# A four-layer graph network on one core: first factor, first products and second factor of the last layer are placed anew

## The chip, the cores and the metric

One core of a Trainium2 chip runs one program with five engines that work at once, each through its own list of instructions in order: PE (TensorE, matrix products into PSUM), DVE (VectorE), ACT (ScalarE), POOL (GpSimd) and SP (SyncE, which here only issues loads). PSUM has eight banks of 2 KB per partition; a bank holds 512 numbers of 32 bits for each of 128 partitions. The metric is the device time of the program in microseconds, as the median of several runs.

## The reference, cut to what matters

Four graph layers on 4096 nodes with 64 features and one dense 4096 x 4096 adjacency matrix, each followed by a residual sum and a layer norm: a Chebyshev layer, an attention layer with two gated cells, a decay layer and a hyperbolic layer. The change lies between the last two:

```python
# layer 2: the last 100 neighbours of a row, weighed by halves
rank = jnp.cumsum(mask, axis=1)
k = jnp.minimum(rank[:, -1:], 100.)
pos = rank - (rank[:, -1:] - k)
w = mask * jnp.where(pos > 0, 0.5 ** (k - pos), 0.0)
x = layernorm(x + w @ (x @ weight) + bias)
# layer 3: log map of every node j at every node i, summed over the neighbours
log_ij = logmap(x[:, None, :], x[None, :, :])     # per pair: a norm, an arctanh
agg = jnp.einsum('ij,ijc->ic', adj / deg, log_ij)
x = layernorm(x + expmap(0, agg @ weight + bias))
```

The log map of a pair depends on one number v(i, j), a product of a vector made from x[i] and one made from x[j]; from it follow an arctanh and a square root, made with logarithms and exponentials.

## The kernel before, in words

Rows are taken in eight groups of 512 columns (`GW`), each group being four blocks of 128 nodes. The matrix is transposed on PE in the first layer and kept in device memory (`adj_t`) with a mask (`mask_t`).

**Decay layer** (loop at L1431). It runs in two turns of four groups, groups 4 to 7 first. In each turn PE goes down through 64 half blocks, with four count matmuls per half block (L1450) into the two banks `cnt_ps` of the pool `ps_c2`; ScalarE (L1455), or VectorE for one of two when no other work is queued (`busy`; L1457), turns the counts into bit patterns of powers of two, `wt`; then PE gathers with them into the four banks `acc_ps` (L1410, L1422). Behind the last gather of a turn `copies` (L1476) takes the four sums from PSUM by VectorE (L1479). What ends a group of rows is cut into steps in the list `seam`, one of which is taken per block pair: `ends` (L1343) makes for two groups the product with the weights (L1360, eight matmuls into a `post` bank), the sum and statistics (L1364 to L1372), the root by logarithm (L1375), the norm (L1380 to L1393), then `prepare` (L1271) and `turn_prepared` (L1289), which leave the transposed columns `tr_c`, `tr_o`. The steps of the first turn run beside the second turn; those of the second turn run in the last layer.

**Last layer** (from L1509). The pairs (i, j) of groups with j not before i in the sequence 4, 5, 6, 7, 0, 1, 2, 3 (`seq`) make 36 tiles, each of two halves: 72 half tiles n. For each group i a pair of **right factors** is made once by `right(i)` (L1526): four matmuls of `tr_c` with `to_right` (L1531) and four of `tr_o` with `to_other` go into two `post` banks, and ScalarE copies them to `rv` and `ro` (L1534). A half tile passes through: `product` (L1577, PE, two banks of `v_ps`), `square` (L1586, ACT), `opposite` (L1596, PE, adds into the same banks), `less_one` (L1604, DVE), Ln and Exp (L1801, L1802, ACT), L1826 (DVE, the last reader of `v_ps`), Exp (L1828) and Ln (L1837, ACT), L1811 and L1814 (DVE, the weight times the matrix entry), transposes for the mirrored tile (L1622, L1624), and gathers into `sums_ps` (L1638, L1650).

The order: `in_order` keeps marked instructions of one engine as written; the rest is placed by a scheduler when the program is built. At the start of the last layer the text has `right(4)`, `product(0)`, `square(0)`, `less_one(0)`, `opposite(0)`, `product(1)`, and then the loop. One or two steps of `seam` are taken per round. `right(5)` comes at round 10, six half tiles ahead of its use.

The pools of PSUM lie one behind another. Decay layer: `ps_c2` two banks, `ps_p2` two (`post`), `ps_a2` four (`acc_ps`). Last layer: `ps_v3` two times two banks (`v_ps`), `ps_a3` two, `ps_p3` two. So the first `v_ps` lies on the counts' banks, the second on the old `post` banks, and the new `post` banks on two of the sums. The matrix `tb` collects finished sums; VectorE fills seven parts of it with zeros at the start (L1544), POOL one (L1542).

Of the kernel before, what the change touches and what calls it, by code (L numbers as in the profile page):

```python
# [9 lines left out]
F32 = mybir.dt.float32  # L10
F32R = mybir.dt.float32r
BF16 = mybir.dt.bfloat16
# [3 lines left out]
ALU = mybir.AluOpType  # L16
AX = mybir.AxisListType
PSUM = bass.MemoryType.PSUM
# [10 lines left out]
V_FLOOR = 2.0**-21  # L29
# [11 lines left out]
SCALE = 2.0**-10  # L41
# [21 lines left out]
def gnn4_kernel(  # L63
# [21 lines left out]
    nc = tc.nc  # L85
    P = 128
    N, F = x.shape
    NB = N // P
    GB = 4
    GW = GB * P  # L90
# [10 lines left out]
    def gcols(g):  # L101
        return slice(g * GW, (g + 1) * GW)
# [264 lines left out]
    wq_signed = const.tile([P, 2, H3], F32, name="wq_signed")  # L367
# [157 lines left out]
    with tc.tile_pool(name="acc", bufs=1) as acc_p, tc.tile_pool(  # L525
        name="cols0", bufs=4
    ) as cols_p, tc.tile_pool(name="kept0", bufs=1) as kept_p, tc.tile_pool(name="diag0", bufs=2) as diag_p, tc.tile_pool(
        name="ps_t0", bufs=3, space=PSUM
    ) as ps_t, tc.tile_pool(name="ps_a0", bufs=1, space=PSUM) as ps_a, tc.tile_pool(
        name="ps_p0", bufs=2, space=PSUM  # L530
# [178 lines left out]
        for g in range(NG):  # L709
# [3 lines left out]
            for c in reversed(range(NCH)):  # L713
# [45 lines left out]
                n = g * NCH + c  # L759
# [55 lines left out]
        for g in reversed(range(NG - 1)):  # L815
            ps = ps_a.tile([P, GW], F32, name="pass2", tag=("h_ps", "w_ps")[g % 2])
# [60 lines left out]


    turns_of = [list(range(NG - QG, NG)), list(range(NG - QG))]

    def load2(to, groups, c):

# [456 lines left out]


    decayed = {}

    def ends(two):  # L1343
# [12 lines left out]
        def summed(ps_p):  # L1356
            o = ps_p.tile([P, GB, 2 * F], F32, name="post", tag="post")
            for b in range(GB):
                for q, g in enumerate(two):
                    nc.tensor.matmul(  # L1360
                        o[:, b, q * F : (q + 1) * F], lhsT=decayed[g][:, cols(b)], rhs=wd, start=True, stop=True
                    )
            halves = "p (q b) f -> p q b f"
            nc.vector.tensor_tensor(  # L1364
                x2.rearrange(halves, q=2), o.rearrange("p b (q f) -> p q b f", q=2),
                nat_b[:, bs, :].rearrange(halves, q=2), ALU.add,
            )
            st = sm.tile([P, 2 * GB, 6], F32, name="ln_st")
            for b in range(2 * GB):
                nc.vector.bn_stats(st[:, b, :], x2[:, b, :])  # L1370
                nc.vector.bn_aggr(mv[:, b, :], st[:, b, :])
            nc.vector.tensor_scalar_add(ve, mv[:, :, 1], LN_EPS)  # L1372

        def roots(ps_p):
            nc.scalar.activation(s, ve, AF.Ln)  # L1375
            nc.scalar.activation(s, s, AF.Exp, scale=0.5)

        def rest(ps_p):

# [12 lines left out]
            nc.vector.tensor_scalar_mul(ve, ve, 1.0 / F)  # L1392
            nc.vector.tensor_tensor(x2, x2, over_all(ve), ALU.subtract)  # L1393

        return [summed, roots, rest, lambda ps_p: prepare(two)] + [
            lambda ps_p, g=g: turn_prepared(ps_p, g) for g in two
        ]

    with tc.tile_pool(name="mask2", bufs=3) as mk_p, tc.tile_pool(name="wt2", bufs=3) as wt_p, tc.tile_pool(
# [31 lines left out]
        for turn, groups in enumerate(turns_of):  # L1431
# [9 lines left out]
            for h in reversed(range(2 * NB)):  # L1441
# [31 lines left out]

                gathers += lo + two if jb == 0 else two + lo
                if jb == 0:
                    def copies(ps_p, acc=acc, groups=groups):  # L1476
                        for q, g in enumerate(groups):
                            decayed[g] = three.tile([P, GW], F32, name=f"sums{q}")
                            nc.vector.tensor_copy(decayed[g], acc[q])  # L1479

                    assert turn == 0 or not seam
                    seam += [lambda ps_p: None, copies]
                    for a in range(2):
                        seam += ends((groups[2 * a], groups[2 * a + 1]))
                busy = bool(seam)
                if seam:
                    seam.pop(0)(ps_p)
# [18 lines left out]

    with tc.tile_pool(name="o3", bufs=1) as op, tc.tile_pool(name="cols3", bufs=3) as cols_p, tc.tile_pool(  # L1509
        name="w3", bufs=4  # L1510
    ) as wp3, tc.tile_pool(name="el3", bufs=3) as el, tc.tile_pool(name="f3", bufs=2) as fp, tc.tile_pool(
        name="r3", bufs=2
    ) as rp, tc.tile_pool(name="ps_v3", bufs=2, space=PSUM) as ps_v, tc.tile_pool(
        name="ps_a3", bufs=2, space=PSUM
    ) as ps_a, tc.tile_pool(name="ps_p3", bufs=2, space=PSUM) as ps_p:
        HB = CB // 2

        tb = op.tile([P, N], F32, name="tb")
# [1 line left out]
        spread_w = two_w[:, F : 2 * F]  # L1520
        kappa = op.tile([P, 2, NB], F32, name="kappa")

        rvs = [op.tile([P, GW], F32, name=f"rv{q}") for q in range(2)]
        ros = [op.tile([P, GW], BF16, name=f"ro{q}") for q in range(2)]

        def right(i):  # L1526
            q = seq.index(i) % 2
            for to, w, t in ((rvs[q], to_right, tr_c), (ros[q], to_other, tr_o)):
                ps = ps_p.tile([P, GW], F32, name="post", tag="post")
                for b in range(GB):  # L1530
                    nc.tensor.matmul(  # L1531
                        ps[:, cols(b)], lhsT=w[:, b % 2, :], rhs=t[:, (i * GB + b) // 2, :], start=True, stop=True
                    )
                nc.scalar.copy(to, ps)  # L1534
            return rvs[q], ros[q]


        seq = turns_of[0] + turns_of[1]
        tiles = [(i, j) for n, i in enumerate(seq) for j in seq[n:]]
        NT = len(tiles)  # L1540
        own, mirrored = {}, {}
        nc.gpsimd.memset(tb[F:P, gcols(seq[0])], 0.0)  # L1542
        for g in seq[1:]:
            nc.vector.memset(tb[0:F, gcols(g)], 0.0)  # L1544

        def load_own(t):
            if t < NT and t not in own:
# [12 lines left out]
            i, j = tiles[n // 2]  # L1560
            return slice(2 * P if i == j and n % 2 else 0, GW)

        rights, sums, fs = {}, {}, {}
        vs, ws, rts = {}, {}, {}
        NU = 2 * NT

        def product(n):

            if n >= NU:
                return  # L1570
            i, j = tiles[n // 2]
            vs[n] = ps_v.tile([P, HB, GW], F32, name="v_ps")
            cs = columns(n)
            for k in range(HB):
                jb = j * CB + (n % 2) * HB + k
                half = slice(jb % 2 * F, jb % 2 * F + F)
                in_order(nc.tensor.matmul(  # L1577
                    vs[n][:, k, cs], lhsT=tr_c[half, jb // 2, :], rhs=rights[i][0][half, cs], start=True, stop=True
                ))

        def square(n):
            if n >= NU:
                return
            ws[n] = wp3.tile([P, HB, GW], F32, name="w3")
            cs = columns(n)
            nc.scalar.activation(ws[n][:, :, cs], vs[n][:, :, cs], AF.Square)  # L1586

        def opposite(n):
            if n >= NU:
                return  # L1590
            i, j = tiles[n // 2]
            cs = columns(n)
            for k in range(HB):
                jb = j * CB + (n % 2) * HB + k
                half = slice(jb % 2 * F, jb % 2 * F + F)
                in_order(nc.tensor.matmul(  # L1596
                    vs[n][:, k, cs], lhsT=tr_o[half, jb // 2, :], rhs=rights[i][1][half, cs],
                    start=False, stop=True, skip_group_check=True,
                ))

        def less_one(n):
            if n < NU:
                w = ws[n][:, :, columns(n)]
                nc.vector.tensor_scalar(w, w, -SCALE * SCALE, V_FLOOR * (V_FLOOR + 2.0) * SCALE**2, ALU.add, ALU.max)  # L1604

        def turn(n):

# [171 lines left out]
        for t in range(3):  # L1779
            load_own(t)  # L1780
            load_mirrored(t)
        rights[seq[0]] = right(seq[0])
        product(0)
        square(0)
        less_one(0)
        opposite(0)
        product(1)
        n = 0
        while n < NU + 2 or turns or gathers:
            if n % 2:  # L1790
# [49 lines left out]
            for _ in range(2 if n == 0 else 1):  # L1840
                if seam:
                    seam.pop(0)(ps_p)
            if n + 6 < NU and tiles[(n + 6) // 2][0] not in rights:
                i = tiles[(n + 6) // 2][0]
                rights[i] = right(i)
            n += 1

        before, last = seam[:-6], seam[-5:]
# [49 lines left out]
```

## Time and profile before

| what | us |
|---|---|
| median of three runs | 1402.75 (1402.37 to 1404.16) |
| the profiled execution | 1408.86, its span 1407.1 |
| first weight load of the decay counts (L1450) | 762.5 |
| sums of the second turn copied from | 963.97 |
| last gather of the decay layer ends | 964.15 |
| busy PE, DVE, ACT, POOL over the span | 1310.2, 1052.1, 805.7, 110.5 |

A line of the chain has the start in the span, the length, the engine and the line. A stretch has its bounds and length, each engine's busy time with the number of instructions, the granted clock of PE as a share of the full one, the share of the DMA engines and their rate. fp32 matmuls are recorded in two passes, so four matmuls are eight records. PE's busy time is modelled and does not mean that its array is full.

### The profile page before, as it was taken

The numbers are of one execution on the slowest core, as the hardware profiler recorded it, in microseconds if no ns is written. First come the engines' busy times: TensorE is split into PE (matmuls) and PEld (weight loads), VectorE is DVE, ScalarE is ACT, GpSimd is POOL, SyncE is SP. The second block draws the span as 40 slices with busy tenths as digits, with TensorE's granted clock in tenths as the row PEclk, the third lists the DMA queues.
The fourth block names the chain that finished last, engine by engine and source line by source line (L and its number), as shares of the span: only waits on it lengthen the run. The fifth ranks groups of instructions, "written<-read, shape, count | busy, mean of one in ns | idle before, by whom it ended". The sixth has DMA issues, their size and how long they took to land.

```text
span 1407.1 us, 19039 instructions
## 1 busy us (share of the span) xinstructions
PE 1310.2 (93%) x6790; PEld 611.1 (43%) x6790; DVE 1052.1 (75%) x2015; ACT 805.7 (57%) x1341; POOL 110.5 (8%) x191
## 2 busy tenths in 40 slices
PE   7999999999999999999999999997889898989893
PEld 5655556556544334444444323333333333333341
DVE  7599889999434257788885224356999999999997
ACT  4544434434000115654424675744989999999894
POOL 2111111011123000010111000000000000000000
PEclk9999999999999999999999999997999999999998
DMA  9999999999799999999985755534244354445330
GB/s 317 392 390 412 376 410 400 405 404 384 290 381 372 388 419 373 421 350 340 329 306 179 239 173 165 181 120 180 78 162 187 149 229 158 184 154 198 138 120 12
DMA packets 108191, 382.16 MB, mean 272 GB/s; under 512 B 20276, under 2 KB 20280, under 8 KB 76472
## 3 DMA queue, kind: packets, MB, share of 16 engines
q1 hardware_dynamic: 87096, 296.17, 57.0%
q0 software_dynamic: 12736, 76.29, 13.2%
q10 hardware_dynamic: 8256, 8.39, 1.7%
q8 instruction: 56, 0.92, 0.3%
q14 instruction: 47, 0.39, 0.1%
HBM read 294.05 MB, written 85.20 MB: 270 GB/s over the span
## 4 chain that ended last, share of the span: by engine, by line
PE 59%; ACT 15%; DVE 15%; DMA 6%; issue 3%; SPq 1%; ACTq 0%; POOL 0%; DVEq 0%
PE pass L566 7%; PE tp L723 6%; PE w_ps L566 6%; PE pass L559 4%; PE cnt_ps L1450 4%; PE a_last L1181 4%; PE a_ps L1181 4%; PE acc_ps L1410 3%; DMA raw<-in_adj_dram 3%; PE h_ps L559 3%; ACT w L1801 2%; ACT rt L1802 2%; DVE rt L1826 2%; ACT w L1586 2%; DVE at_m L1624 2%
## 5 line engine op out<-in xcount | busy, mean ns | idle before, releaser
L730 ACT COPY at<-tp 128x512 f32<-128x512 f32 x248 | 128.5, 598 | 124.2 <-issue 88.6
L1455 ACT ACTIVATE wt<-cnt_ps 128x512 uint16<-128x512 f32 x210 | 116.5, 595 | 65.3 <-PE cnt_ps L1450 63.0
L758 DVE TENSOR_REDUCE dpart<-raw 128x4 f32<-128x2048 f32 x64 | 145.4, 2274 | 4.8 <-DMA raw<-in_adj_dram 4.7
L1638 PE MATMUL sums_ps<-at_d,some 128*64 128x512 f32 x288 | 144.3, 621 | 2.7 <-DVE at_d L1617 1.7
L760 DVE TENSOR_REDUCE lows<-raw 128x1 f32<-128x2048 f32 x64 | 145.4, 2272 | 0.0
L723 PE MATMUL tp<-ident,raw 128*128 128x128 f32 x1024 | 134.4, 285 | 9.8 <-DMA raw<-in_adj_dram 8.3
L723 PEld LDWEIGHTS tp<-ident,raw 128*128 128x128 f32 x1024 | 117.8, 146 | 46.8 <-issue 37.3
L1650 PE MATMUL sums_ps<-at_m,some 128*64 128x512 f32 x224 | 110.0, 613 | 0.0
L1577 PE MATMUL v_ps<-rv,tr_a 64*128 64x512 f32 (+1 forms) x288 | 82.6, 652 | 21.1 <-DVE rt L1826 20.8
L566 PE MATMUL pass<-at,cheb_n 128*128 128x512 f32 x224 | 97.5, 593 | 0.5 <-DVE cheb_n L792 0.5
L566 PE MATMUL w_ps<-at,cheb_n 128*128 128x512 f32 x200 | 91.8, 602 | 0.0
L1826 DVE SCALAR_TENSOR_TENSOR rt<-v_ps,rt 128x1024 f32<-128x1024 f32 x72 | 83.2, 1156 | 5.3 <-ACT rt L1802 4.7
L1450 PE MATMUL cnt_ps<-m,follow 128*64 128x512 fp8e4 x480 | 81.7, 391 | 4.6 <-ACT wt L1455 1.5
L1814 DVE TENSOR_TENSOR at_d<-at_d,f 128x1024 f32<-128x1024 f32 x72 | 83.2, 1156 | 0.1
L1811 DVE SCALAR_TENSOR_TENSOR f<-rt,w 128x1024 f32<-128x1024 f32 x72 | 83.1, 1158 | 0.2 <-ACT rt L1837 0.2
L1624 DVE TENSOR_TENSOR at_m<-post,at_m 128x512 f32<-128x512 f32 x112 | 74.9, 680 | 8.6 <-PE post L1622 8.4
L1837 ACT ACTIVATE rt<-rt 128x1024 f32<-128x1024 f32 x72 | 72.1, 1005 | 11.4 <-DVE rt L1826 10.8
L1457 DVE TENSOR_SCALAR wt<-cnt_ps 128x512 uint16<-128x512 f32 x46 | 31.8, 692 | 59.0 <-PE cnt_ps L1450 59.0
L1801 ACT ACTIVATE w<-w 128x1024 f32<-128x1024 f32 x72 | 72.0, 1000 | 6.5 <-DVE w L1604 6.4
L1622 PE MATMUL post<-ident,f 128*128 128x128 f32 x448 | 68.9, 284 | 4.8 <-DVE at_m L1624 4.5
L1828 ACT ACTIVATE w<-w 128x1024 f32<-128x1024 f32 x72 | 72.4, 1006 | 0.6
L1802 ACT ACTIVATE rt<-w 128x1024 f32<-128x1024 f32 x72 | 72.4, 1005 | 0.6
(426 smaller groups left out, 2279.7 us busy)
## 6 DMA issues: line engine op xcount, KB each, us to landing
at<-adj_t SPq DMA_DIRECT2D x119, 1024.0 KB, 8.5
raw<-in_adj_dram SPq DMA_DIRECT2D x64, 1024.0 KB, 13.3
adj_t<-at POOLq DMA_DIRECT2D x62, 1024.0 KB, 8.2
at_d<-adj_t SPq DMA_DIRECT2D x36, 1024.0 KB, 4.6
at_m<-adj_t SPq DMA_DIRECT2D x28, 1024.0 KB, 6.7
m<-mask_t SPq DMA_DIRECT2D x120, 128.0 KB, 2.9
m<-mask_t SPq DMA_DIRECT2D x60, 256.0 KB, 4.2
mask_t<-mask ACTq DMA_DIRECT2D x28, 256.0 KB, 7.5
```

Source lines behind the costliest of these rows:

```text
L566: in_order(nc.tensor.matmul(ps, lhsT=cheb_n[:, jb, k : k + 2, :], rhs=rhs, start=first, stop=last))
L723: in_order(nc.tensor.transpose(tp[:, cols(b)], raw[:, b, cols(k)], ident))
L730: nc.scalar.copy(at[:, k, :], tp)
L758: in_order(nc.vector.tensor_reduce(dpart[:, g, c, :], raw, AX.X, ALU.add))
L760: in_order(nc.vector.tensor_reduce(lows[:, n : n + 1], raw.rearrange("p b j -> p (b j)"), AX.X, ALU.min))
L1181: in_order(nc.tensor.matmul(ps[q * F : (q + 1) * F, :], lhsT=nat_a[:, c * CB + k, 0:F], rhs=of[q if signed else 0][:, k, :], start=(c == 0 ...
L1450: in_order(nc.tensor.matmul(cnt[a][r * HP : (r + 1) * HP, :], lhsT=follow, rhs=chunks[c][odd][2 * a + r][:, k, :], start=(h == 2 * NB - 1) ...
L1455: in_order(nc.scalar.activation(wt[odd][a], cnt[a], AF.Relu, scale=-128.0))
L1624: work.append(lambda to=to, tp=tp: nc.vector.tensor_tensor(to, tp, to, ALU.mult))
L1638: in_order(nc.tensor.matmul(bank[0:F, :], lhsT=nat_c[:, j * CB + k, :], rhs=own[t][:, k, :], start=(i == j and k == 0), stop=(j == seq[-1] ...
L1650: in_order(nc.tensor.matmul(bank[F:P, :], lhsT=nat_c[:, above * GB + k, :], rhs=mirrored[tm][:, k, :], start=(k == 0 and above == seq[0]), ...
L1826: nc.vector.scalar_tensor_tensor(rt, vs[n][:, :, cs], (1.0 + V_FLOOR) * SCALE, rt, ALU.max, ALU.add)
```

## The change

1. `right(seq[0])` is made in the decay layer, as the last step of `seam` in the first turn. Its results lie in places that are there already: `rv` in the unused quarter of the tile `some`, the first `ro` in the weights `wq_signed`. `right` takes the pool as an argument.
2. The pools of the last layer are ordered `ps_v3` (one buffer, two banks: the counts'), `ps_p3` (the old `post` banks), `ps_u3` (one buffer, two banks: sums 0 and 1), `ps_a3` (sums 2 and 3). Even half tiles use `ps_v3`, odd ones `ps_u3`.
3. In the second turn sums 2 and 3 are copied by ScalarE.
4. The order at the start: `product(0)`, `square(0)`, `product(1)`, `less_one(0)`, `opposite(0)`. `behind` makes the first row-end matmuls stand behind the first products and the first `opposite` on PE, and the row-end sum behind `less_one(0)` on DVE, by an edge for the scheduler that is no wait.
5. `right(seq[1])` moves from round 10 to round 0, behind the row-end products.
6. The seven fills of `tb` go to POOL.

```diff
+    rights, begun = {}, {}
+    rvs = [some[:, N // 4 + q * GW : N // 4 + (q + 1) * GW] for q in range(2)]
+    ros = [wq_signed.rearrange("p q h -> p (q h)")[:, 0 : GW // 2].bitcast(BF16)]
+    def right(ps_p, i):
+        q = seq.index(i) % 2
+        for to, w, t in ((rvs[q], to_right, tr_c), (ros[q], to_other, tr_o)):
...
+        rights[i] = rvs[q], ros[q]
+    def behind(engine, ins):
+        if engine in begun:
+            tc.add_manual_dep(
+                ins.ins, begun[engine],
+                mybir.DependencyInfo(mybir.DependencyClass.NoSync, mybir.DependencyReason.DATA),
+                reason="behind",
+            )
+        begun[engine] = ins.ins.name
@@ ends: row-end products and sum @@
+                    if begun:
+                        behind("PE", ins)
...
+            if begun:
+                behind("DVE", ins)
@@ decay layer @@
-                            nc.vector.tensor_copy(decayed[g], acc[q])
+                            copy = nc.scalar.copy if turn and q > 1 else nc.vector.tensor_copy
+                            copy(decayed[g], acc[q])
...
+                    if turn == 0:
+                        seam.append(lambda ps_p: right(ps_p, seq[0]))
@@ last layer @@
-        name="r3", bufs=2
-    ) as rp, tc.tile_pool(name="ps_v3", bufs=2, space=PSUM) as ps_v, tc.tile_pool(
-        name="ps_a3", bufs=2, space=PSUM
-    ) as ps_a, tc.tile_pool(name="ps_p3", bufs=2, space=PSUM) as ps_p:
+    with tc.tile_pool(name="ps_v3", bufs=1, space=PSUM) as ps_v, tc.tile_pool(
+        name="ps_p3", bufs=2, space=PSUM
+    ) as ps_p, tc.tile_pool(name="ps_u3", bufs=1, space=PSUM) as ps_u, tc.tile_pool(name="o3", bufs=1) as op, tc.tile_pool(name="cols3", bufs=3) as cols_p, tc.tile_pool(
...
-            nc.vector.memset(tb[0:F, gcols(g)], 0.0)
+            nc.gpsimd.memset(tb[0:F, gcols(g)], 0.0)
...
-            vs[n] = ps_v.tile([P, HB, GW], F32, name="v_ps")
+            vs[n] = (ps_u if n % 2 else ps_v).tile([P, HB, GW], F32, name="v_ps")
...
+                if n < 2:
+                    behind("PE", ins)
...
+                if n < 1:
+                    behind("PE", ins)
...
+                if n < 1:
+                    behind("DVE", ins)
...
-        rights[seq[0]] = right(seq[0])
         product(0)
         square(0)
+        product(1)
         less_one(0)
         opposite(0)
-        product(1)
...
+            if n == 0:
+                right(ps_p, seq[1])
             if n + 6 < NU and tiles[(n + 6) // 2][0] not in rights:
                 i = tiles[(n + 6) // 2][0]
-                rights[i] = right(i)
+                right(ps_p, i)
```

More of the change, by code (lines that the diff above doesn't have):

```diff
@@ L879, in gnn4_kernel @@
     turns_of = [list(range(NG - QG, NG)), list(range(NG - QG))]
+    seq = turns_of[0] + turns_of[1]
     def load2(to, groups, c):
@@ L1341, in gnn4_kernel @@
     decayed = {}
+    rights, begun = {}, {}
[4 more added lines that the diff above has]
+        for to, w, t in ((rvs[q], to_right, tr_c), (ros[q], to_other, tr_o)):
+            ps = ps_p.tile([P, GW], F32, name="post", tag="post")
+            for b in range(GB):
+                nc.tensor.matmul(
+                    ps[:, cols(b)], lhsT=w[:, b % 2, :], rhs=t[:, (i * GB + b) // 2, :], start=True, stop=True
+                )
+            nc.scalar.copy(to, ps)
+        rights[i] = rvs[q], ros[q]
[5 more added lines that the diff above has]
+                reason="behind",
+            )
+        begun[engine] = ins.ins.name
     def ends(two):
@@ L1359, in summed @@
                 for q, g in enumerate(two):
-                    nc.tensor.matmul(
+                    ins = nc.tensor.matmul(
                         o[:, b, q * F : (q + 1) * F], lhsT=decayed[g][:, cols(b)], rhs=wd, start=True, stop=True
                     )
+                    if begun:
+                        behind("PE", ins)
             halves = "p (q b) f -> p q b f"
-            nc.vector.tensor_tensor(
+            ins = nc.vector.tensor_tensor(
                 x2.rearrange(halves, q=2), o.rearrange("p b (q f) -> p q b f", q=2),
@@ L1475, in gnn4_kernel, with copies @@
                 if jb == 0:
-                    def copies(ps_p, acc=acc, groups=groups):
+                    def copies(ps_p, acc=acc, groups=groups, turn=turn):
                         for q, g in enumerate(groups):
                             decayed[g] = three.tile([P, GW], F32, name=f"sums{q}")
-                            nc.vector.tensor_copy(decayed[g], acc[q])
+                            copy = nc.scalar.copy if turn and q > 1 else nc.vector.tensor_copy
+                            copy(decayed[g], acc[q])
                     assert turn == 0 or not seam
@@ L1493, in gnn4_kernel @@
     staying.close()
-    with tc.tile_pool(name="o3", bufs=1) as op, tc.tile_pool(name="cols3", bufs=3) as cols_p, tc.tile_pool(
+    with tc.tile_pool(name="ps_v3", bufs=1, space=PSUM) as ps_v, tc.tile_pool(
+        name="ps_p3", bufs=2, space=PSUM
+    ) as ps_p, tc.tile_pool(name="ps_u3", bufs=1, space=PSUM) as ps_u, tc.tile_pool(name="o3", bufs=1) as op, tc.tile_pool(name="cols3", bufs=3) as cols_p, tc.tile_pool(
         name="w3", bufs=4
@@ L1512, in gnn4_kernel @@
         name="r3", bufs=2
-    ) as rp, tc.tile_pool(name="ps_v3", bufs=2, space=PSUM) as ps_v, tc.tile_pool(
+    ) as rp, tc.tile_pool(
         name="ps_a3", bufs=2, space=PSUM
-    ) as ps_a, tc.tile_pool(name="ps_p3", bufs=2, space=PSUM) as ps_p:
+    ) as ps_a:
         HB = CB // 2
@@ L1521, in gnn4_kernel @@
         kappa = op.tile([P, 2, NB], F32, name="kappa")
[L1523 to L1538, printed above, removed]
         tiles = [(i, j) for n, i in enumerate(seq) for j in seq[n:]]
@@ L1561, in columns @@
             return slice(2 * P if i == j and n % 2 else 0, GW)
-        rights, sums, fs = {}, {}, {}
+        sums, fs = {}, {}
+        ros.append(op.tile([P, GW], BF16, name="ro1"))
         vs, ws, rts = {}, {}, {}
@@ L1576, in product @@
                 half = slice(jb % 2 * F, jb % 2 * F + F)
-                in_order(nc.tensor.matmul(
+                ins = nc.tensor.matmul(
                     vs[n][:, k, cs], lhsT=tr_c[half, jb // 2, :], rhs=rights[i][0][half, cs], start=True, stop=True
-                ))
+                )
+                in_order(ins)
+                if n < 2:
+                    behind("PE", ins)
         def square(n):
@@ L1595, in opposite @@
                 half = slice(jb % 2 * F, jb % 2 * F + F)
-                in_order(nc.tensor.matmul(
+                ins = nc.tensor.matmul(
                     vs[n][:, k, cs], lhsT=tr_o[half, jb // 2, :], rhs=rights[i][1][half, cs],
                     start=False, stop=True, skip_group_check=True,
-                ))
+                )
+                in_order(ins)
+                if n < 1:
+                    behind("PE", ins)
         def less_one(n):
@@ L1603, in less_one @@
                 w = ws[n][:, :, columns(n)]
-                nc.vector.tensor_scalar(w, w, -SCALE * SCALE, V_FLOOR * (V_FLOOR + 2.0) * SCALE**2, ALU.add, ALU.max)
+                ins = nc.vector.tensor_scalar(
+                    w, w, -SCALE * SCALE, V_FLOOR * (V_FLOOR + 2.0) * SCALE**2, ALU.add, ALU.max
+                )
+                if n < 1:
+                    behind("DVE", ins)
         def turn(n):
```

## The prediction

> **What bounds the kernel now.** I read the order of time first, to find where the decay layer hands over to the last layer, since the change touches only that passage; then the chain of waits there; then the engines' busy time in short stretches on either side.
>
> The chain between 963 and 977 us (start, length, what):
> ```profile
> 963.98 0.28 DVE sums L1479
> ...
> 964.58 1.89 DVE sums L1479 x3
> ...
> 966.51 1.17 PE post L1531 x8
> ...
> 967.75 0.59 ACT rv L1534
> ...
> 968.39 2.08 PE v_ps L1577 x4
> 970.46 3.62 PE post L1360 x16
> 974.10 0.07 DVE nat_a L1364
> ...
> 974.71 0.69 DVE w L1604
> 975.43 1.06 ACT w L1801
> ```
> The reader is to see one work after another: four copies empty the decay sums, then the first right factor is made, copied, used by the first product, then sixteen matmul records of the row ends go ahead, and only then VectorE does the step that lets ScalarE take its first logarithm, at 975.43. The last gather into the sums ended at 964.15 (963.77 + 0.38 in the order of time), so 11.3 us pass.
>
> The stretches (us, then busy PE, weight loads, DVE, ACT, POOL; granted clock; DMA share; GB/s):
> ```profile
> 960.00:964.00 4.00, 4.00 (x40) 1.44 (x37) 1.42 (x4) 1.20 (x2) 0.00 (x0) 1.00 0.00 0
> 964.00:968.00 4.00, 1.64 (x14) 1.27 (x12) 3.84 (x7) 0.25 (x1) 0.52 (x1) 0.95 0.66 248
> 968.00:972.00 4.00, 3.67 (x13) 2.11 (x12) 2.06 (x6) 1.85 (x3) 0.00 (x0) 0.50 1.01 422
> 972.00:976.00 4.00, 3.46 (x16) 2.68 (x16) 1.90 (x9) 0.57 (x1) 0.00 (x0) 0.50 1.02 426
> 976.00:980.00 4.00, 1.10 (x4) 0.60 (x5) 3.59 (x17) 4.00 (x9) 0.00 (x0) 0.50 1.01 418
> 1000.00:1020.00 20.00, 17.15 (x90) 8.06 (x88) 19.97 (x46) 18.97 (x22) 0.00 (x0) 1.00 0.23 81
> 1100.00:1200.00 100.00, 90.59 (x429) 36.59 (x428) 96.41 (x155) 96.29 (x132) 1.56 (x2) 1.00 0.45 171
> ```
> Before the passage PE is full. In it nothing is. After it DVE and ACT are both near full, DVE fullest (19.97 of 20 us), and they stay so to the end. So a start made earlier is kept as far as DVE's work comes earlier. The clock falls to half at 967.7 and returns at 991.5.
>
> **The change part by part.** The built order of the changed kernel says what moves; durations are from the rows of before, on its profiled execution (span 1407.1, time 1408.86, so 6.1 above the median 1402.75; the difference is carried to the median).
>
> *First right factor in the decay layer.* Twelve matmul records and two ScalarE copies move to the step behind the last row end there. The same work in the last layer at full clock starts its first eight records 1.13 before the next row, and the four bf16 ones 0.32 (1034.51 and 1036.71): 1.45. PE is full in that layer (19.76 of 20 in 900 to 920), so it is paid. One more step also has ScalarE doing all four count conversions in place of two; such a step took 2.95 with 0.59 of row-end transposes on PE, a plain one 2.74, so nothing is added for that. Elsewhere in that layer 2.35 us of mask loads stand on the chain (916.60), and such a wait could hide it: ends 0 and 2.7 (1.54, the factor's matmuls at 966.51, plus two copies of 0.59). I take **+1.4**, nearest to the row of the same matmuls.
>
> *The start of the last layer.* The two product tiles now lie in the counts' banks and in those of sums 0 and 1. Product 0 waits for no copy and no factor, product 1 for two DVE copies; the two other copies go to ACT. Taking 964.15 as it is, at full clock (the table has start and end):
>
> | engine | step | us |
> |---|---|---|
> | PE | product 0 (1.06 at 995.38) | 964.2–965.3 |
> | DVE, ACT | two copies each (0.62; 0.48 start to start, 0.59) | to 965.3 |
> | PE | product 1, half the columns | 965.3–965.9 |
> | ACT | squares 0 and 1 (1.02, 0.58) | 965.4–966.9 |
> | DVE | L1604 for 0 and 1 (0.69, 0.43) | 966.45–967.45 |
> | PE | opposites, 16 row-end records (4.4 us for 32), second factor | 966.45–970.65 |
> | ACT | Ln, Ln, Exp | 967.15–969.65 |
> | DVE | L1364, half the statistics, L1826 | 969.25–971.8 |
> | ACT | copy of factor 2 (idle 0.75 for PE), Exp, copy, Exp, Ln | 970.4–973.9 |
> | DVE | other statistics, mean off, L1826, L1811, L1604 | 971.8–975.75 |
>
> So the logarithm of the third half tile starts near 975.75; in the chart of before it starts at 983.54: 7.8 earlier. But by then DVE in before had done five small row-end steps (0.7) and L1386 (0.6) which are still to come: 7.8 − 1.3 = **−6.5**. What is late next is DVE, which then has no gap. The second factor is behind the row ends on PE, and on ACT its copy stands ahead of Exp: three ACT steps, and DVE's L1811, wait out its 0.75. Bounds of this sum: if PE ran at half clock all through, the posts would take 3.67 in place of 2.2 and the factor 1.1 more: −6.5 + 2.5 = −4. At the other end nothing but ACT counts: −7.8.
>
> *Seven fills of tb go from DVE to POOL* (3.73 us on DVE, now at most 8 x 0.52 on POOL to about 968.6). In before they lay ahead of a wait of 3.83 for PE and cost nothing; their absence is in the table. Behind them on POOL are fills for the second row ends, some 10 us later, so nothing waits. No row has a POOL fill beside L1604, so its cost is bounded by nothing and by one fill, 0.52; I take 0, since the one POOL fill of before ran beside copies that kept their 678 to 693 ns, though these read PSUM. The Trainium skill, "SBUF — State Buffer", section "SBUF: two separate sides", speaks against this: it says that GpSimd and a VectorE operation in a two-port mode lock each other out for a whole instruction. By that rule L1604 would be held up by one fill and the sum would be 0.5 worse; no run here shows it yet.
>
> *Second factor no longer made at step 10.* There ACT waited 1.07 for it (1035.71) and PE gave 1.45; DVE was the bound there (28.5 of 30). Ends 0 and −1.4; I take **−0.6**.
>
> *Loads.* The queue of SP is unchanged. The second own tile landed 6.7 us after its issue (about 971.5), the third after 12.1 (977.8). The first is multiplied at 984.17 now and would be at about 976: covered. With more than 8 us gained the second would be next.
>
> *Pools, places of the factors, order helpers:* no instruction, 0.
>
> Sum: +1.4 − 6.5 − 0.6 = **−5.7**: 1408.86 becomes 1403.2 in a profiled execution, and the median 1402.75 becomes **1397.0**.
>
> **The rivals.**
>
> *A. The clock falls during the start.* It fell with PE busy 1.2 of the 3.4 us before; in the table PE is busy for nearly all of 964.2 to 970.65, so against. If it did: −4 + 1.4 − 0.6 = −3.2, **1399.5**.
>
> *B. The clock does not fall at all.* After 970.65 PE waits for L1826 and works some 1.3 of 4 us, like the drop above, so I expect the fall near 974. The clock changes nothing before it in my sum. If it held, the half-clock pieces on the later chain (2.08 and 2.61 us at 987.92 and 990.00) would shrink by 2.3: −8.0, **1394.7**. The Trainium skill, "TensorE: Matmul & The Clock Gate", section "Why this matters for your kernels", asks for an idle gap of more than about 3 us for a drop; the gaps here would be shorter, so by it B holds. The trace disagrees: the clock fell after a gap of 2.36.
>
> *C. The clock returns no earlier than 991.* It needed 24 us in before. PE at half clock for 8 us more loses 4 us of work just where it is on the chain: −5.7 + 4, **1401.0**.
>
> *D. Slower: the steady stage loses its clock more often.* The order of PE's instructions is new up to about step 16, and with ACT and DVE full, PE idles in short gaps. Before had three drops after 1000 us, of one window each (3.4 to 3.75 us; 1022.0, 1059.5, 1312.25), each worth at most half its length, 1.8. Five more would be +9: −5.7 + 9 = +3.3, **1406.0**. It decides from the fifth on; against it, the last 300 us keep their order.
>
> That the change would not do what it says is excluded by the built order: the first products stand right behind the last gather, and the row-end sums behind the opposites.
>
> **How the numbers follow.** Forecast 0.52, A 0.14, B 0.16, C 0.10, D 0.08. A measurement of this kernel can tell about 0.2% (2.8 us) from no change: 1399.95 to 1405.55. Faster: 0.50 of the forecast, half of A, B: 0.73. Same: the rest of A and of the forecast, nearly all of C: 0.19. Slower: D: 0.08. The range reaches from B with both cheap ends (0 for the decay layer, −1.4 at step 10), about 1392.5, to C with the 0.52 of a fill beside L1604, 1401.5; outside it are D and about a tenth more.
>
> **What would show it.** Right: last gather about 1.4 later than 964.15; first Ln 3 to 3.5 us behind it in place of 11.3; no wait of DVE above 2 us up to the third L1604; clock at 1.0 until about 970 us. Wrong: row-end records of above 0.2 us each (A); PE on the chain after the passage for more than 8 us (C); more than three drops after 1000 (D); PE in the decay layer longer by 2.7. A load of the first own tile on the chain would break the table.

## The result and the profile after

The changed kernel takes 1397.76 us (median of 6 runs, 1395.76 to 1399.74) beside 1402.56 for the kernel before (6 runs, 1398.84 to 1404.16): ratio 0.997, 95% interval 0.9956 to 0.9985. In a second set of runs on one chip the ratio was 0.9955 (0.9937 to 0.9973). The two sets put the gain at 4 to 6 us (2 to 9 us by their intervals).

The profiled execution took 1395.76, its span 1394.0, against 1407.1 before. Of these 13.1 us, 7.1 lie before the first emptying of the decay sums (at 868.46 before and 861.33 after), where nothing was changed; all twelve later profiles have that mark at 860 to 865, so the profile of before was a long one. From here on I count from marks. The **decay stretch** goes from the first sums copy of the first turn to that of the second; the **tail** from there (963.97 before, 958.57 after) to the end. A logarithm is ScalarE's Ln of one half tile (L1801 before, L1829 after).

The chain of waits of the changed kernel through the passage (start, length, what):
```profile
957.78 0.97 PE acc_ps L1439 x8
958.75 0.89 PE v_ps L1596 x4
...
959.86 0.94 ACT w L1608
...
960.84 0.39 PE v_ps L1618 x2
961.23 0.36 PE post L1385 x2
961.60 0.21 PE v_ps L1618 x2
961.81 1.72 PE post L1385 x14
...
963.55 0.70 DVE nat_a L1391
```
The product (L1596) now stands right behind the last gather; the opposite products (L1618) come ahead of 14 of the 16 row-end records, which take 0.12 us each in place of 0.23. The chain reaches the row-end sum (L1391) 4.8 us after the last gather; before it took 10. The first and the third logarithm of the changed kernel start at 961.63 and 970.32:
```profile
961.63 1.06 ACT L1829 ACTIVATE w<-w 128x1024 f32<-128x1024 f32 x1 [0.24 <-DVE w L1629]
...
970.32 1.06 ACT L1829 ACTIVATE w<-w 128x1024 f32<-128x1024 f32 x1 [0.18 <-DVE w L1629]
```

The stretches (us, then busy PE, weight loads, DVE, ACT, POOL; granted clock; DMA share; GB/s):
```profile
960.00:964.00 4.00, 3.86 (x30) 3.14 (x31) 2.09 (x4) 3.76 (x5) 3.72 (x7) 1.00 0.98 379
964.00:968.00 4.00, 1.81 (x13) 0.89 (x12) 3.93 (x21) 3.66 (x8) 0.00 (x0) 1.00 1.01 420
...
972.00:976.00 4.00, 2.21 (x6) 0.63 (x5) 4.00 (x12) 4.00 (x5) 0.00 (x0) 0.73 0.79 326
1100.00:1200.00 100.00, 90.92 (x433) 36.81 (x430) 96.53 (x140) 96.78 (x129) 1.56 (x2) 1.00 0.47 180
```
From 964 on DVE is nearly full (3.93 of 4 us, later 4.00); in the kernel before it is so only from about 976 on (3.59 of 4), some 12 us after the passage began. The clock is full until 973.9 and half for 3.4 us, in place of the 24 us of before.

Here are the marks of all kernels (us; logarithms counted from the start of the tail). The last two columns are the way from the first sums copy to the 17th logarithm, less that of before (196.56), and the measured ratio to the kernel before.

| kernel | decay stretch | log. 1 | log. 3 | log. 11 | 11 to 17 | way | ratio (95%) |
|---|---|---|---|---|---|---|---|
| before | 95.51 | 11.46 | 19.57 | 65.95 | 35.10 | 0 | 1 |
| changed | 97.24 | 3.06 | 11.75 | 58.70 | 35.31 | -5.3 | 0.9970 (0.9956-0.9985) |
| e1 no hoist | 95.52 | 4.95 | 13.72 | 60.68 | 35.31 | -5.0 | 0.9956 (0.9941-0.9972) |
| e2 hoist alone | 97.22 | 6.84 | 16.90 | 62.90 | 36.07 | -0.4 | 0.9990 (0.9980-1.0000) |
| e3 hoist, fills | 97.22 | 3.51 | 12.23 | 59.69 | 38.12 | -1.5 | 0.9987 (0.9975-1.0000) |
| e4 before, 16 idle | 95.52 | 13.31 | 21.42 | 68.82 | 38.67 | +6.5 | 1.0036 (1.0023-1.0049) |
| e5 second at 10 | 97.22 | 3.06 | 11.68 | 58.69 | 38.38 | -2.3 | 0.9972 (0.9960-0.9985) |
| e6 fills late | 97.23 | 3.06 | 12.30 | 59.85 | 36.59 | -2.9 | 0.9965 (0.9951-0.9979) |
| e7 no order | 97.21 | 3.07 | 11.86 | 58.81 | 35.32 | -5.2 | 0.9960 (0.9943-0.9976) |
| e8 before, 5 idle | 95.52 | 8.84 | 16.94 | 64.29 | 38.61 | +1.9 | 1.0002 (0.9986-1.0019) |
| e9 changed again | 97.22 | 3.06 | 11.74 | 58.69 | 36.58 | -4.1 | 0.9955 (0.9937-0.9973) |
| e10 fills late, mended | 97.22 | 2.98 | 11.75 | 58.70 | 35.32 | -5.3 | 0.9936 (0.9913-0.9959) |
| e11 second early | 95.52 | 8.84 | 17.92 | 63.34 | 34.58 | -3.1 | 0.9977 (0.9964-0.9991) |
| e12 half hoist | 96.75 | 2.98 | 11.75 | 58.77 | 34.58 | -6.5 | 0.9950 (0.9932-0.9968) |

One execution of e1 (4990.87 us) and one of before (7038.37) are left out of the ratios. The way of one profile and the timed ratio tell nearly the same story: 1% is 14 us, so 0.9977 is -3.2 beside -3.1 for e11, 0.9990 is -1.4 beside -0.4 for e2. The two agree within 2.3 us for all kernels but e10 (-5.3 beside -9.0, from four executions). A single tail is a poorer measure: it ends 1 to 3 us apart for equal starts, by where the clock falls later on.

### The profile page after: what moved, and what is told of

It reads as the page before. It is cut to its first block, busy times and chain, and to the rows that moved or that the text cites. A ratio compares the mean times of both kernels' runs of the same rounds, so it can differ in the third digit from the quotient of the medians.

```text
span 1394.0 us, 19042 instructions
## 1 busy us (share of the span) xinstructions
PE 1295.1 (93%) x6790; PEld 603.8 (43%) x6790; DVE 1046.3 (75%) x2004; ACT 807.7 (58%) x1345; POOL 114.2 (8%) x198
## 4 chain that ended last, share of the span: by engine, by line
PE 57%; DVE 16%; ACT 15%; DMA 7%; issue 3%; SPq 1%; ACTq 0%; POOL 0%; DVEq 0%
PE pass L566 7%; PE w_ps L566 6%; PE tp L723 6%; DMA raw<-in_adj_dram 6%; PE a_ps L1182 4%; PE pass L559 4%; PE cnt_ps L1479 4%; PE a_last L1182 4%; PE acc_ps L1439 3%; PE p_ps L1173 2%; ACT w L1829 2%; ACT rt L1830 2%; DVE rt L1854 2%; ACT w L1608 2%; PE h_ps L559 2%
## 5 line engine op out<-in xcount | busy, mean ns | idle before, releaser
L723 PE MATMUL tp<-ident,raw 128*128 128x128 f32 x1024 | 130.6, 280 | 10.4 <-DMA raw<-in_adj_dram 9.1
L723 PEld LDWEIGHTS tp<-ident,raw 128*128 128x128 f32 x1024 | 114.3, 143 | 47.3 <-issue 34.1
L1596 PE MATMUL v_ps<-some,tr_a 64*128 64x512 f32 (+1 forms) x288 | 78.1, 619 | 24.0 <-DVE rt L1854 23.2
L1829 ACT ACTIVATE w<-w 128x1024 f32<-128x1024 f32 x72 | 72.0, 1001 | 2.8 <-DVE w L1629 2.8
## 6 DMA issues: line engine op xcount, KB each, us to landing
raw<-in_adj_dram SPq DMA_DIRECT2D x64, 1024.0 KB, 13.1
```

What stands on the lines that cost most here:

```text
L723: in_order(nc.tensor.transpose(tp[:, cols(b)], raw[:, b, cols(k)], ident))
```

## The experiments

**e1, without the hoist.** The first factor goes back to the head of the last layer; all else is as changed.
```
-                    if turn == 0:
-                        seam.append(lambda ps_p: right(ps_p, seq[0]))
...
+        right(ps_p, seq[0])
         product(0)
```


> The changed kernel with one part undone: the first right factor is made at the start of the last layer again, ahead of the first product; banks, order and fills stay as changed. Marks: the decay stretch (first sums copy of the first turn to that of the second) was 95.5 us before and 97.2 after; the tail (from there to the end) 443.1 and 435.4; the first logarithm began 11.5 and 3.1 us into the tail. Theory (the order of the start makes the gain, and the hoist only trades): the decay stretch falls back to 95.5; the factor's matmuls take 1.45 at the head of the tail and its copy follows the two ScalarE sums copies, so the first product starts 1.9 later, the first logarithm at 4.9, the tail is 437.3; in sum +0.2 against the changed kernel (1397.5 to 1398.5). Rival (taking the factor off the chain is what makes the gain): the tail goes back by 4 or more, to 439.5, and the time to 1400 or above.

The decay stretch fell by 1.72, the first logarithm came 1.89 later (4.95), the 17th 1.98 later; the time is not to be told from the changed kernel's (0.9956 beside 0.9970 and 0.9955). The hoist is a trade at par. The tail, 439.9, would have spoken for the rival, but 2.6 of its 4.5 us came after the 31st logarithm, with clock drops at 1336 and 1366 that the first profile of the changed kernel lacks.

**e2, the hoist alone, and e3, hoist and fills.** The kernel before with `right(ps_p, seq[0])` in the decay layer's list of steps; e3 has in addition
```
-            nc.vector.memset(tb[0:F, gcols(g)], 0.0)
+            nc.gpsimd.memset(tb[0:F, gcols(g)], 0.0)
```


> The kernel before with only the first right factor moved into the decay layer; pools, copies, fills, second factor and order as before. Theory: the decay stretch grows by 1.7; the first product can start at once, but VectorE has four copies (2.5) and seven fills (3.7) ahead of its first step, which now cost, since nothing hides them: first logarithm at 7 us into the tail, the third at 16 to 17 in place of 19.6, tail shorter by 3 to 4, in sum -1 to -2.5. Rival (the factor is the whole of it): first logarithm at 3 to 4 us, tail shorter by 7 or more, the whole gain of the change.

> The kernel of the run before this (first factor in the decay layer, the rest as before), with the seven fills of tb moved from VectorE to GpSimd as well. Theory: the fills were hidden before only by the wait for TensorE; here they come off the path: first logarithm at 3.5 us into the tail, but the second tile's product still stands behind the row-end records: tail 436.5 to 438, that is 2 to 3 us better than without the move. Rival (fills never matter): tail and logarithms as in the run before, within 0.5.

VectorE in e2 and then in e3, the start of the last layer (start, length, engine, line, operation):
```profile
959.04 2.48 DVE L1495 COPY sums<-acc_ps 128x512 f32<-128x512 f32 x4 [1.24 <-PE acc_ps L1426]
961.57 3.73 DVE L1546 MEMSET tb<- 64x512 f32 x7
965.23 0.62 DVE L1606 TENSOR_SCALAR w<-w 128x1024 f32<-128x1024 f32 x1
```
```profile
959.82 2.49 DVE L1495 COPY sums<-acc_ps 128x512 f32<-128x512 f32 x4 [1.25 <-PE acc_ps L1426]
...
962.32 0.97 DVE L1606 TENSOR_SCALAR w<-w 128x1024 f32<-128x1024 f32 x1
```
In e2 the seven fills (3.73) stand between the copies and the first step; in e3 the step follows the copies. So fills that cost nothing in the kernel before, where a wait of 3.83 covered them, cost 3.3 at the first logarithm and 3.2 at the 11th once the factor is gone from the chain. The time does not show it: the medians, 1402.33 and 1401.98, are 0.4 apart, and 1.1 of the 3.2 is left at the 17th logarithm. e2 came out as expected. e3 had the start expected, but its tail was 441.8, not 436.5 to 438, and the 2 to 3 us expected of the move are missed: between the 11th and 17th logarithm it lost 2.8 us against the changed kernel. That stretch is taken up with e5.

Beside e1, e3 also shows that two parts of the change do one job. At the 11th logarithm hoist and fills alone are 6.3 us ahead of before, everything but the hoist 5.3, the whole change 7.3: what is added second brings 1 to 2 us. The banks and the two copies on ScalarE were not taken back by themselves in any run.

**e4 and e8, the start of the kernel before with TensorE kept busy.** The diff is e4's; e8 has 5 in place of 16. Their results are overwritten by the first product.
```
+        for k in range(16):
+            in_order(nc.tensor.matmul(
+                vs[0][:, k % 2, 0 : 2 * P], lhsT=to_right[:, 0, :], rhs=tr_c[:, m : m + 2, :], start=True, stop=True
+            ))
         rights[seq[0]] = right(seq[0])
         product(0)
```


> The kernel before with 16 idle f32 matmuls (into the first product's own bank, overwritten by it) right behind the last gather, where TensorE waited for the four copies; they change no result. Rival (the gain of the change is that the clock no longer stays at half for 24 us): the clock holds through the passage, and the tail falls by 6 or more, to below 437. Theory (the order of the start): the half clock's part is the first product (2.08 to 1.06) and the sixteen records (3.62 to 2.2), so the first logarithm comes 2 to 2.5 earlier, at 9.0 to 9.5, and the tail falls by 2 to 3, to 440 to 441. If the clock falls all the same, nothing moves.

> The kernel before with 5 idle f32 matmuls (ten records, 2.3 us) right behind the last gather, in the gap in which TensorE waited for the four copies (with 16 of them, 7.2 us, the gap was overrun and the factor came 4.6 late, but from the factor's start to the row-end sum's end took 4.9 in place of 7.6 at the held clock). Theory (order of the start; the clock is a part): the clock holds to about 968 us or longer, the first logarithm comes at 8.7 to 9.3 us into the tail, the third at 17, the tail is shorter by 2 to 3: 440 to 441. Rival (the gain is the clock): tail below 437.

I had counted e4's 16 matmuls as 16 records; they were 32 of 0.22 us, 7.17 in all, and put the factor 4.6 late. e8 is the clean one: first logarithm 8.84 and third 16.94, as expected, so the half clock's share of the start was 2.6 us in that profile. But 1.0 of it was lost by the 11th logarithm, the tail was 443.3 in place of the 440 to 441 expected, and the time did not move (1.0002). Of the 7.25 us that the changed kernel is ahead at the 11th logarithm the clock in the start is 1.7 by this profile, or 2.6 if what was lost again is counted; the larger part is the order of the start.

**e5, the second factor back at step 10.**
```
-            if n == 0:
-                right(ps_p, seq[1])
```


> The changed kernel with the second right factor made at step 10 again; all else as changed. The prediction priced its removal from step 10 at -0.6 and its presence in the start inside the -6.5. Theory: without it ScalarE has two copies less in the start, so the third logarithm comes about 1 earlier than 11.75 us into the tail, and steps 10 to 16, which took 35.3 in the changed kernel, take 1 to 2 more; decay stretch 97.2; tail 435.4 to 437; in sum 0 to +1.5 against the changed kernel. Rival (its place is worth nothing): tail 435.4 within 0.4. Rival (a copy of a factor in step 10 costs the clock as well, as in the runs with the factor there): steps 10 to 16 take 38, a drop of the clock of two windows near 1034, tail 438.

The third logarithm came 0.07 earlier, not 1: two copies and 1.45 us of TensorE more in the start cost nothing there. The 11th to 17th logarithm took 38.38, as the last rival said. TensorE in e5, and then the same place in the changed kernel:
```profile
1030.19 0.30 PE L1708 MATMUL post<-ident,spread 128*64 128x128 f32 x1
1032.25 0.68 PE L1712 MATMUL post<-wh,spread_t 64*128 64x64 f32 x2 [1.76 <-DVE spread_t L1710]
```
```profile
1028.14 0.30 PE L1708 MATMUL post<-ident,spread 128*64 128x128 f32 x1 [0.35 <-DVE at_m L1653]
1028.37 0.39 PE L1618 MATMUL v_ps<-wq_signed,some 64*128 64x512 bf16 x2
1029.86 1.13 PE L1596 MATMUL v_ps<-some,tr_a 64*128 64x512 f32 x4 [1.10 <-DVE rt L1854]
1030.83 0.33 PE L1712 MATMUL post<-wh,spread_t 64*128 64x64 f32 x2
```
With the factor in step 10 the build puts the transpose of `spread` (the `weights` step) straight ahead of the matmul that needs its copy: TensorE waits 1.76 us for VectorE with all its work behind it. Without the factor two products lie between, and the copy is hidden. All six kernels with the factor in step 10 (before, e2, e3, e4, e5, e8) have this wait of 1.76, and none of the other eight. And in five of the six the clock falls 14 to 17 us after the 11th logarithm, for one or two spells; in none of the eight. The granted clock there, e5 and then the changed kernel (columns as above):
```profile
1028.00:1032.00 4.00, 1.71 (x7) 0.50 (x6) 4.00 (x6) 4.00 (x5) 0.00 (x0) 0.96 0.01 2
1032.00:1036.00 4.00, 3.75 (x10) 1.26 (x10) 3.58 (x8) 2.59 (x3) 0.00 (x0) 0.50 0.00 0
1036.00:1040.00 4.00, 4.00 (x18) 2.21 (x18) 2.21 (x3) 3.36 (x4) 0.00 (x0) 0.69 0.62 207
```
```profile
1026.00:1030.00 4.00, 2.55 (x15) 1.20 (x15) 3.19 (x8) 3.27 (x5) 0.00 (x0) 1.00 0.01 2
1030.00:1034.00 4.00, 4.00 (x24) 1.89 (x24) 3.96 (x9) 3.98 (x5) 0.00 (x0) 1.00 0.01 2
```
The clock of e5 is at half from 1031.7 to 1038.5: PE becomes full, and DVE, which bounds the layer, falls to 3.58 and then 2.21 of 4 us. The one execution of these six without the drop is the profile of before itself, from which I predicted. No run keeps the factor in step 10 and takes only the wait away; that the wait brings the drop is made likely by a count in the last section, and not shown by a run.

**e11, the second factor early, alone.** The kernel before with
```
+            if n == 0:
+                rights[seq[1]] = right(seq[1])
```


> The kernel before with only the second right factor moved from step 10 to the start, behind the first row-end records. Theory (the factor at step 10 opens a gap for TensorE after which the clock falls between 1031 and 1041, in most executions): steps 10 to 16 take 35.1 to 35.4 without such a drop; the start is later by the factor's 1.45 and two copies at half clock, third logarithm 20.5 to 22 us into the tail in place of 19.6; in sum the time is that of before within 2 us. Rival (step 10 costs nothing): steps 10 to 16 as they were, drops or not, and the time 1 to 2.5 above before for the later start.

The 11th to 17th logarithm took 34.58 without a drop, and the time fell to 0.9977, by the median more than either theory allowed: this line alone brings 1.3 to 5.1 us. Against before, which had no drop in the stretch either (35.10), it saves 0.5 there; more than that it can save there only where the clock would have dropped. Against e8, whose start up to the first logarithm is as long (8.84), its third logarithm is 1.0 later, its 11th 0.95 earlier, its 17th 5.0 earlier. (Some of the 5.0 is not of step 10: e8 has a drop from 1017.3 to 1024.2, around its 11th logarithm, as e6 and e9 have without the factor in step 10, and their stretch took 36.6 with it. The third logarithm was forecast at 20.5 to 22 and came at 17.92, since the start held the clock; see the last section.) With all the rest of the change in place, e5 against the changed kernel, the line is worth 3 us on the way and 0 to 2.4 by the medians of the ratios.

**e7, without the manual orders.**
```
-        if engine in begun:
+        if engine in ():
```


> The changed kernel without the orders that hold the row-end records behind the opposite products and the row-end sum behind the first VectorE step; with the factor and the banks as changed, only four of the sixteen records go ahead of the first opposite product and four between the two. Theory: the order was already nearly right once the first product waits for nothing; first logarithm at 3.1, third within 0.5 of 11.75, tail within 0.6 of 435.4. Rival (the order is a main part of the gain): first logarithm 1 or more later, tail 437 or more.

The marks and the time are as the theory had it: logarithms 0.01 to 0.11 later, the time that of the changed kernel. The tail, 438.1, is outside the 0.6 allowed, but 2.6 of its 2.7 us came after the 31st logarithm, with clock drops at 1335 and 1366 as in e1. Once the product waits for nothing, the build's own order is nearly the one written out.

**e6 and e10, GpSimd's fills held behind VectorE's first steps.** The fills move behind a one-column copy that reads the second step's output; in e10 a manual order keeps the copy ahead of the fills.
```
+                behind("POOL", nc.gpsimd.tensor_copy(first_w, ws[1][:, 0, GW - 1 : GW]))
+                behind("POOL", nc.gpsimd.memset(tb[F:P, gcols(seq[0])], 0.0))
+                for g in seq[1:]:
+                    behind("POOL", nc.gpsimd.memset(tb[0:F, gcols(g)], 0.0))
```


> The changed kernel with the eight GpSimd fills held behind VectorE's first two steps (a one-column GpSimd copy of the second step's output goes ahead of them), so that none lies beside these. Theory (a fill and a VectorE step on SBUF alone hold each other up): the first two steps take 0.69 and 0.43 in place of 0.82 and 0.78, the seven fills 3.3 in place of 4.2, the second logarithm comes 0.2 to 0.5 earlier, the tail is 435.0 to 435.4. Rival (the longer steps have another cause): they keep 0.8 each. The time can't tell these apart; the rows can.

> The run with the late fills, mended: there the eight fills went ahead of the one-column copy on GpSimd, the copy came last and the second logarithm waited for it. Now the copy is held ahead of the fills. Theory (a fill and a VectorE step on SBUF alone hold each other up): the first two VectorE steps take 0.69 and 0.43, the seven fills 3.3 to 3.4, the second logarithm comes at 3.5 to 3.85 us into the tail and the third at 11.3 to 11.75. Rival (another cause): the two steps keep 0.82 and 0.78.

e6 tested something else: there the build put the copy last, and the second logarithm, which overwrites what it reads, waited until 5.31; that cost 1.15 at the 11th logarithm. e10 did what was meant. VectorE and GpSimd in the changed kernel, then in e10:
```profile
960.82 1.52 DVE L1629 TENSOR_SCALAR w<-w 128x1024 f32<-128x1024 f32 x2 [0.69 <-ACT w L1608]
...
963.55 0.69 DVE L1391 TENSOR_TENSOR nat_a<-post,tr_a 128x512 f32<-128x512 f32 x1 [1.22 <-PE post L1385]
...
959.56 4.16 POOL L1562 MEMSET tb<- 64x512 f32 x7
```
```profile
960.93 1.03 DVE L1626 TENSOR_SCALAR w<-w 128x1024 f32<-128x1024 f32 x2 [0.86 <-ACT w L1605]
963.66 0.69 DVE L1391 TENSOR_TENSOR nat_a<-post,tr_a 128x512 f32<-128x512 f32 x1 [1.70 <-PE post L1385]
963.14 3.32 POOL L1873 MEMSET tb<- 64x512 f32 x7
```
Side by side the two steps take 1.52 and the seven fills 4.16; apart 1.03 and 3.32. Each holds the other up. But what VectorE saves, 0.49, its next wait gives back: 1.70 in place of 1.22. The third logarithm stays at 11.75 to the hundredth; the second comes at 3.94 in place of 4.03, where 3.5 to 3.85 was forecast. The time, 0.9936, is the lowest of all, but its interval holds the 0.9955 of the changed kernel on the same chip, so no gain is shown.

**e9, the changed kernel again.**


> The changed kernel once more, word for word, timed beside the next three on one chip and profiled a second time, to see what one profile's tail is worth. Theory: decay stretch 97.2, first logarithm 3.1 and third 11.75 us into the tail as in the first profile, since no drop of the clock falls there; steps 10 to 16 take 35.3 without a drop; the tail is 435.4 plus 0.9 to 3 for each drop of the clock in the steady stage that the first profile did not have: 435 to 439. Rival (the tail is set by the instructions alone): 435.4 within 0.2.

Equal instructions gave the same marks to 0.02 up to the 11th logarithm, and then 36.58 in place of 35.31, for a drop of 6.8 us at 1015.9 where the first profile had one of 3.4 at 1014.8. The half clock after the passage lasted 10.2 us in place of 3.4 and moved no logarithm up to the 11th.

**e12, a version made from this.** e10, with the bf16 half of the first factor made in the last layer behind the first product and copied by VectorE.
```
+        right(ps_p, seq[0], (1,), nc.vector.tensor_copy)
```


> A version made from what the runs showed: the changed kernel with the late fills as mended, and of the first right factor only the f32 half (1.13 of 1.45 us of TensorE) in the decay layer; the bf16 half is made behind the first product, where TensorE waited 0.4 for a copy, and copied by VectorE, which stood idle. Theory: decay stretch 96.8 to 96.9; first logarithm 3.1, third 11.4 to 11.8 us into the tail; in sum 0.4 to 0.9 better than the changed kernel, too little to be told from it by time. Rival (the bf16 half delays the first opposite product and the row ends): third logarithm at 12 to 12.5, and nothing won.

As expected: the decay stretch is 0.47 to 0.49 shorter, the third logarithm unmoved, and the time, 0.9950, beats the kernel before but can't be told from the changed one. It has the shortest way of all, -6.5, of which 0.7 is a drop of the clock near 1015 that this execution lacked.

## Why the prediction was right, step by step

It gave 1397.0 in 1392.5 to 1401.5; the median is 1397.76. The order of the start was the right mechanism and its term nearly the right size; the term for step 10 lacked the clock drop, and the clock in rivals B and C was mispriced. That the sum came within 0.8 us is closer than its parts deserve, and to that extent luck: the measured gain is known only to 2 to 9 us, which hides a miss of 2 to 3 us in one term.

- **First factor in the decay layer, +1.4:** +1.72. The twelve records cost their 1.45. Of the rest, the extra step with ScalarE alone converting took 2.90 (half-steps of 1.52 and 1.38) against 2.74; I had put that at nothing; 0.1 stays unexplained. e1 shows what I did not ask: the term on the other side of the trade is 1.9, so this part brings nothing.
- **Start of the last layer, -6.5 (-7.8 at the third logarithm):** the third logarithm came 7.82 earlier. The debt of row-end steps, 1.3 in the sum, was 0.6: the 11th logarithm is 7.25 earlier. First logarithm 2.9 behind the last gather (3 to 3.5 forecast); VectorE's longest wait 1.24 (below 2). The third step ended 11.54 after the last gather, 11.6 in the table.
- **Fills, 0 (bound 0.52):** 0 in the sum, although the fills do lengthen the steps by 0.49 (e10). What the Trainium skill, "SBUF — State Buffer", section "SBUF: two separate sides", says of the lock agrees with the trace: of the seven fills in the changed kernel the two that lay beside the steps took 1.06 and 0.80 us, the others 0.52 to 0.57. What it does to the time was decided by the wait behind it. That the fills had to move was the other half: on VectorE they cost 3.2 us at the 11th logarithm (e2, e3), which the medians of those two do not confirm.
- **Second factor off step 10, -0.6 (bounds 0 and -1.4):** the mis-sized term. I priced its own matmuls and copies, and for an execution without a drop the size is right: 35.10 in before, 34.58 in e11. What it also does is displace the transpose of `spread`, which leaves a wait of 1.76 on TensorE, and mostly a clock drop of 3.4 or 6.8 us; e11 measures -3.2 (-5.1 to -1.3) for it alone. The profile of before, the one execution without that drop, hid it: it showed 35.10 for the stretch where e2, with a drop of 3.4, took 36.07, and e3 and e5, with 6.8, took 38.1 and 38.4. (e4 and e8 took 38.7 and 38.6 with 3.4 us of it, but had a second drop around the 11th logarithm.)
- **Rivals.** A did not happen. B and C priced a clock that returns or stays away at 2.3 and 4 us; e9 shows that half clock for 10.2 or 3.4 us there moves nothing, since VectorE is the bound. So B was wrong in mechanism, and C as far as 10 of its 24 us go; no profile of the changed kernel had the clock at half for longer. D: two and three drops after 1000 in the two profiles, three before; no sign of it.

What stays open: how much of the 4 to 6 us belongs to the start and how much to step 10, since the clock falls in either place of the kernel before in some executions and not in others. By the count of the last section I estimate that it falls in the start in some six to nine of ten executions; at step 10 it fell in five of the six profiles. By the way up to the 17th logarithm e5 (all but step 10) gives -2.3 and e11 (step 10 alone) -3.1, but 2.6 of this 3.1 lie ahead of the 11th logarithm, where the start of e11 held the clock and that of before did not.

## What to carry to other kernels

A moved piece costs or gains also by what the scheduler puts in its place: compare the order of neighbouring small steps (a transpose, its copy, its use) and look for a wait of TensorE with a full queue behind it. Work that is free because it lies under a wait, such as the fills here, gets its price back on the day the wait goes, so it has to move in the same change. And where one engine has no gap, count marks on that engine from a fixed event: here they repeated to 0.02 us up to the 11th logarithm, while the spans of the same kernel were 1394.0 and 1397.1.

## What the runs showed of the hardware

The same gap of TensorE ended once in a clock drop and once not. The kernel before, then e11, which has the same instructions up to there:
```profile
966.51 1.16 PE L1531 MATMUL post<-tr_a,to_right 128*128 128x128 f32 x8 [2.36 <-DVE sums L1479]
...
968.39 2.08 PE L1577 MATMUL v_ps<-rv,tr_a 64*128 64x512 f32 x4 [0.33 <-ACT rv L1534]
```
```profile
961.18 1.16 PE L1531 MATMUL post<-tr_a,to_right 128*128 128x128 f32 x8 [2.36 <-DVE sums L1479]
...
963.06 1.13 PE L1577 MATMUL v_ps<-rv,tr_a 64*128 64x512 f32 x4 [0.50 <-ACT rv L1534]
```
After 2.36 us of idle time the product took 2.08 in one execution and 1.13 in the other.

The traces show why. In each of the 14 all changes of the granted clock lie on one grid of steps of 3.41 us, and the grid lies elsewhere in every execution; a drop lasts one, two, three, four, five or seven steps (3.4, 6.8, 10.2, 13.7, 17.1, 23.9 us). For every step of these grids from 940 to 1380 us I counted the share in which TensorE was busy:

| at the start of the step | busy share in the step | steps | clock after it |
|---|---|---|---|
| full clock | below 0.45 | 31 | half in all 31 |
| full clock | 0.45 to 0.60 | 76 | half in 30 |
| full clock | 0.60 or more | 1597 | full in all |
| half clock | below 0.85 | 37 | half in all |
| half clock | 0.88 or more | 63 | full in 60 |

Earlier in the traces, from 30 to 940 us, such steps are few and much alike: of those begun at full clock, 9 of 11 below 0.45 and none of 3698 with 0.60 or more were followed by half clock. So what counted here was the busy share of a whole step, not the length of one gap. Here are the steps of before and of e11 in which the gap lay (columns as above, on the bounds of each grid):
```profile
964.17:967.58 3.41, 1.07 (x10) 1.06 (x11) 3.25 (x6) 0.00 (x0) 0.52 (x1) 1.00 0.65 240
```
```profile
956.73:960.15 3.42, 2.09 (x24) 0.74 (x17) 2.18 (x4) 0.41 (x1) 0.52 (x1) 1.00 0.17 22
960.15:963.56 3.41, 1.89 (x14) 1.50 (x16) 3.14 (x7) 1.07 (x2) 0.00 (x0) 1.00 0.86 344
```
In before one step took in the whole gap: busy 0.31, and the clock fell at its end. In e11 a bound of the grid cut the gap in two, the shares were 0.61 and 0.55, and the clock held. The same count bears on step 10: with the wait of 1.76 us there, stretches of 3.41 us come down to a busy share of 0.48, and for about eight of ten places of the grid a step is below 0.53; in the eight kernels without it none comes below 0.57. By the table the clock can fall at either share; the lower one makes it likelier. TensorE's busy time is modelled, so the bounds of the shares are rough.

The Trainium skill, "TensorE: Matmul & The Clock Gate", section "What's actually happening", tells of a window of 3.41 us that runs free of the kernel; the grid agrees with it, and so does a gap that counts or not by where the window lies. The gap of more than about 3 us that its section "Why this matters for your kernels" asks for was not needed: none of the 61 drops that began in those steps had an idle gap of 3 us or more, and four had none above 0.7.
